# Block 0 of an adaptive-LayerNorm transformer kernel: loads, LayerNorm 1 and queue order rearranged

## The chip, the cores and the metric

One core of a Trainium2 chip runs the whole program. The metric is the device time of one execution in microseconds (us); smaller is better. Three executions of the kernel before took 597.66, 599.33 and 599.54 us, median 599.33.

Names used below: PE is TensorE (matrix products), with PEld its weight loads; DVE is VectorE; ACT is ScalarE; POOL is GpSimd; SP is SyncE, which here only issues DMA transfers. PSUM is the memory that PE writes its sums to, in banks; SBUF is the memory that all engines read.

## The reference

All tensors are float32. `x` is (2, 2048, 512), `cond_1024` is (2, 512).

```python
emb = jnp.dot(jax.nn.silu(t), ada_w) + ada_b
shift_msa, scale_msa, gate_msa, shift_mlp, scale_mlp, gate_mlp = jnp.split(emb, 6, axis=-1)
norm = _ln(x) * (1.0 + scale_msa[:, None]) + shift_msa[:, None]
h = jax.nn.gelu(jnp.dot(norm, ssm_w1) + ssm_b1, approximate=False)
ssm_out = jnp.dot(h, ssm_w2) + ssm_b2
x = x + gate_msa[:, None] * ssm_out
norm2 = _ln(x) * (1.0 + scale_mlp[:, None]) + shift_mlp[:, None]
hf = jax.nn.gelu(jnp.dot(norm2, ff_w1) + ff_b1, approximate=True)
ff_out = jnp.dot(hf, ff_w2) + ff_b2
x = x + gate_mlp[:, None] * ff_out
```

`_ln` subtracts the mean and divides by sqrt(variance + 1e-6) along the last axis.

## The kernel before

The 4096 tokens are cut into 8 blocks of 512. Each block goes through four matrix products: `hA` (w1, 512 to 512), `oA` (w2, 512 to 512, added to x), `hC` (fw1, 512 to 1024) and `oC` (fw2, 1024 to 512, added to x). `hA` and `oA` of a block are each done by a seven-product scheme: instead of eight products of half-size blocks there are seven, P1 to P7, on sums and differences of quarters. The sums of activations are `nS` (for w1's input) and `hSA` (for w2's input); the sums of weights are `w_s` and `fw_s`. Four sums belong to each operand: the first (s0), the second (s1), one written over a quarter in place, and the third (s2). P5 needs s0, P6 needs s1, P7 the quarter in place. For activations of blocks 0 and 1 DVE makes them, for weights POOL does (both L340, two SBUF operands).

PE accumulates P1, P6, P7 and P4 one upon the other in one PSUM bank ("y", tiles `py_...`), P5 and P3 in bank "v" (`pv_...`), P2 in bank "x" (`px_...`); each tag has two buffers. Between two products in the same bank, the earlier result has to be read out (`after` in `hidden` and `residual`) before PE may add the next. `hidden` reads `hA` with the bias b1 added (L594, on DVE, or on ACT when `on_act` is set, L592), adds (L600, L607, L610, on DVE) and applies GELU on ACT. `residual` adds products to x on DVE (L642).

Every engine has one queue and works it in order; the kernel is written under a manual schedule, so the order of the Python statements is the order of each queue. `hooks` (L435) put extra work behind a named product: `hook(hooks, ("P5", "P4"), ops)` runs the first op after P5 is issued and all the rest after P4.

Block 0 starts so. ACT loads four small tables of rows; SP loads x of block 0 in two halves, then `ada_0`, `ada_1` (columns of ada_w for shift and scale, 1 MB each), `w1` (1 MB), `ada_2`, `w2`, gate biases, x of block 1, `ada_3`, `ada_4`, `fw1`. DVE takes mean and variance of the four slots of x (L454, L455), POOL and DVE turn them into `rstd` and `nmr` (`scales`), ACT and DVE normalize two slots each (`normal`, L494 and L498) into `blocks`; PE transposes them (L523); ACT and DVE apply shift and scale (`modulate`, L537 and L539) into `nT`. The shift and scale come from `modulation`: 16 small products on PE (L267, tile `pada`), a transposition (L283) and an addition (L287) on DVE. `gate_rows_of(2)` does the same for the gate (pada_2, `grows`, L295), `first_ssm_gate` spreads it over partitions on PE (`pgate`, L302), `fold2` multiplies w2 by it on DVE (L388) and then makes w2's sums on POOL, and `biases` adds gate times b2 (`gb`) to the four slots of x on POOL (L654).

In the result the order on PE in block 0 is: pada_0, pada_1, 16 transposes, P1, P2, pada_2, P5, pgate, P6, P3, P7, pada_3, P4 of `hA_0`; then P1, P2, P5, P6, pada_4, P7, P3, P4 of `oA_0`, with the transposes of block 1 around P4; then `hA_1`, whose order is P1, P2, P5, P6, pada_5, P7, P3, P4.

Of the kernel before, what the change touches and what calls it, by code (L numbers as in the profile page):

```python
# [36 lines left out]
F32 = mybir.dt.float32  # L37
AF = mybir.ActivationFunctionType
ALU = mybir.AluOpType
EPS = 1e-06  # L40
# [100 lines left out]
def kernel(  # L141
# [29 lines left out]
    const = ctx.enter_context(tc.tile_pool(name="const", bufs=1))  # L171
# [14 lines left out]
    G = 32  # L186
# [3 lines left out]
    R_COND, R_ADA = 0, B * KD  # L190
# [3 lines left out]
    def big_tile(name):  # L194
        return big.tile([P, KD, D], F32, tag="big", name=name)
# [8 lines left out]

    ada = {}

    def load_ada(g):
        ada[g] = big_tile(f"ada_{g}")
        nc.sync.dma_start(
            out=ada[g], in_=ada_w[:, g * D : (g + 1) * D].rearrange("(k p) n -> p k n", p=P)  # L210
        )

    def load_w(name, w, t=None, eng=nc.sync):
        if t is None:
            t = const.tile([P, w.shape[0] // P, w.shape[1]], F32, tag=name, name=name)
        eng.dma_start(out=t, in_=w.rearrange("(k p) n -> p k n", p=P))
        return t
# [13 lines left out]
    ident = const.tile([P, P], F32, tag="ident", name="ident")  # L231
    make_identity(nc, ident)
    load_x(0, 2)
    load_ada(0)
    load_ada(1)
    w1_sb = load_w("w1", w1)
    load_ada(2)

    nc.gpsimd.memset(brows[:, :2, :P], 0.0)
# [12 lines left out]
    b2_bc = work.tile([P, D], F32, tag="gb", name="gb2_0", bufs=2)  # L252
# [3 lines left out]
    load_ada(4)  # L256
    fw1_sb = load_w("fw1", fw1)

    mods = {}

    def rows_of(g):

        pa = ps_g.tile([P, D], F32, tag="x", name=f"pada_{g}")
        w = ada[g].rearrange("p k (n m q) -> p k m n q", n=KD, q=G)
        for k in range(KD):
            for m in range(P // G):
                nc.tensor.matmul(  # L267
                    pa[m * G : (m + 1) * G, :P],
                    silu[:, k, :],
                    w[:, k, m],  # L270
                    start=(k == 0),
                    stop=(k == KD - 1),
                    tile_position=(0, m * G),
                    skip_group_check=True,
                )
        return pa

    def modulation(g0, part):

        g = g0 + part  # L280
        pa = rows_of(g)
        turned = pa[:, P : 2 * P]
        nc.vector.transpose(turned, pa[:, :P])  # L283
        turned = turned.rearrange("p (n q) -> p n q", n=KD)
        m = const.tile([P, KD, B], F32, tag=f"mod_{g0}_{part}", name=f"mod_{g0}_{part}")
        bias = colsT[:, R_ADA + g * KD : R_ADA + (g + 1) * KD]
        nc.vector.tensor_tensor(m, turned[:, :, :B], bias.unsqueeze(2).to_broadcast([P, KD, B]), ALU.add)  # L287
        mods[g0, part] = m

    gate, gate_rows = {}, {}  # L290

    def gate_rows_of(g, tag):
        pa = rows_of(g)
        r = work.tile([P, P] if g == 2 else [P, D], F32, tag=tag, name=f"grows_{g}", bufs=1)
        nc.vector.tensor_tensor(r[:, :P], pa[:, :P], gate_b[g], ALU.add)  # L295
        gate_rows[g] = r
# [138 lines left out]
    def hook(hooks, places, ops):  # L435

        for n, op in enumerate(ops):
            hooks.setdefault(places[min(n, len(places) - 1)], []).append(op)


    class Norm:
# [17 lines left out]
        def scales(self, on_dve=False):  # L459
# [20 lines left out]
            v.tensor_tensor(self.nmr, self.mv[:, :, 0], self.rstd, ALU.mult)  # L480
            v.tensor_scalar(self.nmr, self.nmr, -1.0, None, ALU.mult)  # L481

        def blocks(self):
            return work.tile([P, C, KD, C, Q], F32, tag="blocks", name=f"blocks{self.name}")

        def normal(self, c, eng=None, on_pe=False):

            if c == 0:
                self.nT = big_tile(f"nT{self.name}")
                self.xn = self.blocks().rearrange("p m k c q -> p m (k c q)") if on_pe else self.nT  # L490
            t = self.xn[:, c, :]
            x_c = xs[self.i][:, c, :]
            if eng is None:
                nc.scalar.activation(  # L494
                    t, x_c, AF.Identity, bias=self.nmr[:, c : c + 1], scale=self.rstd[:, c : c + 1]
                )
            else:
                eng.tensor_scalar(  # L498
                    t, x_c, self.rstd[:, c : c + 1], self.nmr[:, c : c + 1], ALU.mult, ALU.add
                )  # L500
# [150 lines left out]
    def biases(i, gb):  # L651

        return [
            lambda c=c: nc.gpsimd.tensor_tensor(xs[i][:, c, :], xs[i][:, c, :], gb, ALU.add)  # L654
            for c in range(C)
        ]
# [9 lines left out]

    forms = const.tile([P, 16, C, HT // C], F32, tag="forms", name="forms")

    hA_0 = forms[:, :8].rearrange("p n a r -> p (n a r)").rearrange("p (k t) -> p k t", k=KD)

    def sums_of_registers(program, reg, engs):

# [105 lines left out]
    def run(ops):  # L778
        for op in ops:
            op()  # L780
# [13 lines left out]
    colsT = const.tile([P, ROWS], F32, tag="colsT", name="colsT")  # L794
# [5 lines left out]
    for n in range(IDLE):  # L800
# [3 lines left out]
            idle, ident, ident.unsqueeze(1).to_broadcast([P, C, P]), start=True, stop=True  # L804
        )

    run(n1[0].stats())
    nc.vector.tensor_copy(colsT, pt[:, :ROWS])


    nc.scalar.activation(
# [1 line left out]
        colsT[:, R_COND:R_ADA].rearrange("p (b k) -> p b k", b=B),  # L813
        AF.Silu,
    )

    for g in (1, 4):
        rows_g = colsT[:, R_ADA + g * KD : R_ADA + (g + 1) * KD]
        nc.vector.tensor_scalar(rows_g, rows_g, 1.0, None, ALU.add)

    picks = const.tile([P, P // G, P], F32, tag="picks", name="picks")
    nc.vector.tensor_copy(
        picks, ident.rearrange("p (m q) -> p m q", q=G)[:, :, :1].to_broadcast([P, P // G, P])
    )
    n1[0].scales(on_dve=True)

    w1_ops, w1_sums, _ = weight_of_first("w1", w1_sb)
    run(w1_sums)
    modulation(0, 0)
    for c in range(C):  # L830
        n1[0].normal(c, nc.vector if c % 2 else None, on_pe=True)
    modulation(0, 1)
    pts = {}

    def transposed(k):
        pts[k] = n1[0].transpose(k, ps_g.tile([P, TB], F32, tag="yv"[k % 2], name=f"pt1_0_{k}"))

    for k in range(KD):
        transposed(k)
    for k in range(KD):  # L840
        n1[0].modulate(k, pts[k], nc.vector if k % 2 else None)
    n1_sums = n1[0].summed(nc.vector)
    run(n1_sums[:2])
    load_ada(5)
# [2 lines left out]
    gb, hA = {2: b2_bc}, {}  # L847
# [9 lines left out]
    def fold2(lo, hi):  # L857
        return [lambda k=k: found["w2"][1][k]() for k in range(lo, hi)]

    hooks = {}  # L860
    hook(hooks, ("P1",), n1_sums[2:3])
    hook(hooks, ("P2",), [lambda: gate_rows_of(2, "grows")] + n1_sums[3:])
    st = n1[1].stats()
    hook(hooks, ("P5",), [ssm_gate, gb2_0] + biases(0, b2_bc) + fold2(0, 1))
    hook(hooks, ("P6",), fold2(1, 7))
    hook(hooks, ("P3", "P7"), st[:2])
    hook(hooks, ("P7",), [lambda: modulation(3, 0)])
    hA[0] = First(0, n1[0].ops, hooks, ("P1", "P2", "P5", "P6", "P3", "P7", "P4"), hA_0)
    w2_ops = found["w2"][0]

    hA_sums = hA[0].summed(nc.vector)
    run(hA_sums[:2])
    hooks = {}
    hook(hooks, ("P1",), hA_sums[2:3] + st[2:] + [n1[1].scales] + fold2(7, 8))
    hook(hooks, ("P2",), hA_sums[3:] + [lambda c=c: n1[1].normal(c, on_pe=True) for c in range(C)])
    hook(hooks, ("P6",), [lambda: modulation(3, 1)])
    hook(hooks, ("P3", "P3", "P4"), n1[1].turned())
    n2 = {0: Norm(0, 2)}
    st = n2[0].stats()
    hook(hooks, ("P3",), st[:2])  # L880
    fw1_ops, fw1_sums, fw1_s = weight_of_first("fw1", fw1_sb)
    hook(hooks, ("P2",), fw1_sums[:1])
    hook(hooks, ("P5", "P4"), fw1_sums[1:3])
    residual("oA_0", 0, hA[0], w2_ops, KD // 2, hooks, order=FIRST)

    def ff_gate():
# [10 lines left out]
    n1_sums = n1[1].summed(nc.vector)  # L897
    run(st[2:3] + n1_sums[:2] + st[3:])
    hooks = {}
# [18 lines left out]
    st = n1[2].stats()  # L918
    hooks = {}
# [15 lines left out]
    hooks = {}  # L935
# [27 lines left out]
    hooks = {}  # L963
# [10 lines left out]
    hooks = {}  # L974
# [6 lines left out]
    hooks = {}  # L981
# [11 lines left out]
    for i in range(1, NBLK):  # L993
        nxt, nx2, last = i + 1 < NBLK, i + 2 < NBLK, i + 1 == NBLK
        hC = Second(i)
        hooks = {}
# [21 lines left out]
        hooks = {}  # L1018
# [16 lines left out]
        hooks = {}  # L1035
# [58 lines left out]
        hooks = {}  # L1094
# [52 lines left out]
```

## Time and profile before

| what | us |
|---|---|
| median of three executions | 599.33 |
| the profiled execution, whole | 597.58 |
| its span, first to last instruction | 595.8 |
| PE busy in it | 588.3 (99%) |
| POOL busy | 395.6 (66%) |
| DVE busy | 372.9 (63%) |
| ACT busy | 220.2 (37%) |

The profile is of one execution. Its times count from the first instruction. The timeline lists instructions in order of time: start, duration, engine, line of the kernel, operation, output and inputs, the count of merged instructions, and in brackets the idle time before and what ended it. An instruction of 128x512 elements works on 128 partitions with 512 numbers each. A float32 matrix product appears as two records; "x8" is one of the seven products of a block. PE's records overlap, since it is pipelined: the next product starts before the one before has left.

Times on which later sections rest, from the transfers' records: x of block 0 landed at 4.72 and 6.36, ada_0 at 9.10, ada_1 at 11.80, w1 at 14.51, ada_2 at 17.23, w2 at 20.67, x of block 1 at 23.87.

### The profile page before, as it was taken

The page shows a single profiled execution, that of the slowest core. Times are in us where ns is not written, and L with a number is a line of the kernel's source. Part 1 is how long each engine was busy: PE and PEld are TensorE (multiplying, and loading weights), DVE is VectorE, ACT ScalarE, POOL GpSimd, SP SyncE. Part 2 cuts the span into 40 slices and gives each one's busy share as a digit, 9 for nine tenths or more (in the row PEclk, how much of TensorE's full clock was granted, in tenths as well). Part 3 has the DMA queues.
Part 4 walks back from the last instruction along what each step waited for, and adds up shares of the span by engine and source line. Part 5 has one row for each costly group of instructions (what it writes and reads, how often), then busy time and mean ns, then how long its engine had stood idle before and what let it go on. Part 6 is the DMA issues. An engine that isn't in the chain of part 4 may idle for free.

```text
span 595.8 us, 8294 instructions
## 1 busy us (share of the span) xinstructions
PE 588.3 (99%) x2875; PEld 510.6 (86%) x2875; DVE 372.9 (63%) x637; ACT 220.2 (37%) x366; POOL 395.6 (66%) x465
## 2 busy tenths in 40 slices
PE   7999999999999999999999999999999999999997
PEld 4888888888888888888888888888888888888886
DVE  4978988897554475555754468643655236458642
ACT  3234437305432364234721356232543235212410
POOL 1878489999853994649967499957975696440300
PEclk9999999999999999999999999999999999999999
DMA  8990332200324105340143601331030400031001
GB/s 319 396 380 11 82 71 82 97 36 35 72 72 136 24 0 136 123 131 1 23 138 70 212 1 45 98 87 55 1 70 2 128 15 2 0 70 73 1 1 71
DMA packets 23702, 50.13 MB, mean 84 GB/s; under 512 B 4544, under 2 KB 5100, under 8 KB 22764
## 3 DMA queue, kind: packets, MB, share of 16 engines
q1 hardware_dynamic: 20624, 45.38, 24.0%
q10 hardware_dynamic: 3036, 4.22, 3.0%
q8 instruction: 23, 0.38, 0.3%
q14 instruction: 19, 0.16, 0.1%
HBM read 26.51 MB, written 8.40 MB: 59 GB/s over the span
## 4 chain that ended last, share of the span: by engine, by line
PE 97%; DMA 2%; DVE 1%; SPq 0%; issue 0%
PE py_oC L420 19%; PE px_hC L741 10%; PE py_oA L420 9%; PE pv_oC L420 9%; PE py_hA L420 9%; PE py_hC L741 8%; PE pv_hC L741 8%; PE pv_oA L420 5%; PE px_oC L420 5%; PE pv_hA L420 4%; PE py_hC L420 2%; PE px_oA L420 2%; PE px_hA L420 2%; DMA ada<-in_L_cond_ada_w_dram 2%; PE pv_hC L420 1%; PE pada L267 1%
## 5 line engine op out<-in xcount | busy, mean ns | idle before, releaser
L654 POOL TENSOR_TENSOR x<-x,gb 128x512 f32<-128x512 f32 x64 | 79.5, 1277 | 5.3 <-issue 2.1
L537 ACT ACTIVATE nT<-nT,mod,mod 128x512 f32<-128x512 f32 x54 | 39.6, 802 | 102.0 <-DMA nT<-blocks 95.9
L463 POOL TENSOR_SCALAR ve<-mv 128x4 f32<-128x4 f32 x16 | 3.7, 232 | 91.7 <-DVE mv L455 85.0
L494 ACT ACTIVATE nT<-x,nmr,rstd 128x512 f32<-128x512 f32 x56 | 42.4, 803 | 52.4 <-POOL nmr L481 36.6
L420 PE MATMUL py_oC<-fw,hClo 128*128 128x256 f32 x256 | 57.9, 379 | 0.0
L420 PEld LDWEIGHTS py_oC<-fw,hClo 128*128 128x128 f32 x256 | 48.6, 190 | 6.6
L642 DVE TENSOR_TENSOR x<-py_oC,x 128x512 f32<-128x512 f32 (+1 forms) x36 | 22.6, 629 | 42.9 <-PE py_oC L420 42.9
L454 DVE BATCH_NORM_STATS2 st<-x 128x6 f32<-128x512 f32 x64 | 43.5, 679 | 5.0 <-DMA x<-in_x_dram 4.7
L340 POOL TENSOR_TENSOR hSC<-hClo,hChi 128x512 f32<-128x512 f32 (+1 forms) x17 | 20.1, 1188 | 39.7 <-ACT hChi L736 29.2
L741 PE MATMUL py_hC<-forms,fw 128*128 128x256 f32 x168 | 40.8, 379 | 0.0
L758 DVE TENSOR_TENSOR hClo<-hClo,py_hC 128x512 f32<-128x512 f32 x42 | 28.5, 681 | 16.9 <-ACT hClo L755 10.4
L505 DVE STREAM_TRANSPOSE blocks<-nT 128x512 f32<-128x512 f32 x56 | 37.8, 694 | 1.3 <-ACT nT L494 0.9
L679 POOL TENSOR_TENSOR forms<-forms 128x256 f32<-128x256 f32 x48 | 35.7, 743 | 2.8
L741 PEld LDWEIGHTS py_hC<-forms,fw 128*128 128x128 f32 x168 | 31.8, 190 | 4.4
L758 DVE TENSOR_TENSOR hChi<-hChi,pv_hC 128x512 f32<-128x512 f32 x35 | 23.3, 683 | 17.1 <-PE pv_hC L741 14.2
L642 DVE TENSOR_TENSOR x<-py_oA,x 128x512 f32<-128x512 f32 x32 | 22.0, 688 | 18.9 <-PE py_oA L420 18.3
L420 PE MATMUL py_hA<-nT,w 128*128 128x256 f32 x128 | 30.4, 380 | 0.0
L736 ACT ACTIVATE hClo<-hClo,colsT 128x256 f32<-128x256 f32 x56 | 25.4, 500 | 10.8 <-DVE hClo L758 10.7
L420 PE MATMUL px_oC<-fw,hChi 128*128 128x256 f32 x128 | 28.9, 379 | 0.0
L420 PE MATMUL py_oC<-fw_s,hSC 128*128 128x256 f32 x128 | 28.9, 379 | 0.0
L420 PE MATMUL pv_oC<-fw,hSC 128*128 128x256 f32 x128 | 28.9, 379 | 0.0
L420 PE MATMUL pv_oC<-fw_s,hSC 128*128 128x256 f32 x128 | 28.9, 379 | 0.0
(213 smaller groups left out, 1424.8 us busy)
## 6 DMA issues: line engine op xcount, KB each, us to landing
nT<-blocks SPq DMA_DIRECT2D x168, 64.0 KB
out_dram<-x SPq DMA_DIRECT2D x15, 512.0 KB
x<-in_x_dram SPq DMA_DIRECT2D x7, 1024.0 KB
ada<-in_L_cond_ada_w_dram SPq DMA_DIRECT2D x6, 1024.0 KB
fw<-in_L_cond_ff_w_dram SPq DMA_DIRECT2D x3, 2048.0 KB
nT<-blocks ACTq DMA_DIRECT2D x56, 64.0 KB
w<-in_L_cond_ssm_w_dram SPq DMA_DIRECT2D x3, 1024.0 KB
x<-in_x_dram SPq DMA_DIRECT2D x2, 512.0 KB
```

Source lines behind the costliest of these rows:

```text
L340: eng.tensor_tensor(out[:, r], a[:, r], b[:, r], f)
L420: nc.tensor.matmul(ps[b][j * apart][:, j, :], lhs(p, j, k), rhs(p, j, k), start=(fresh and j * (not apart) == 0 and k == 0), stop=(p in (" ...
L454: nc.vector.bn_stats(st, xs[self.i][:, c, :])
L494: nc.scalar.activation(t, x_c, AF.Identity, bias=self.nmr[:, c : c + 1], scale=self.rstd[:, c : c + 1])
L505: nc.vector.transpose(self.bl[:, :, :, c, :].rearrange("p m k q -> p k m q"), self.nT[:, c, :].rearrange("p (k m q) -> p k m q", k=KD, m=C),)
L537: nc.scalar.activation(dst, src, AF.Identity, bias=shift, scale=scale)
L642: nc.vector.tensor_tensor(d, ps[BANK[p]][:, js], d, ALU.add)
L654: lambda c=c: nc.gpsimd.tensor_tensor(xs[i][:, c, :], xs[i][:, c, :], gb, ALU.add)
L679: eng.tensor_tensor(reg[d], reg[a], reg[b], ALU.add if f == "+" else ALU.subtract)
L736: nc.scalar.activation(h, h, AF.Gelu_apprx_tanh, bias=fb1T[:, m : m + 1])
L741: nc.tensor.matmul(ps[b][:, j, :], fa[ra][:, j * P : (j + 1) * P], fb[rb].rearrange("p a (c q) -> p c a q", q=Q), start=(fresh and j == 0) ...
L758: nc.vector.tensor_tensor(dest(d), dest(d), ps[b], op)
```

## The change

Loads: `ada_0` and `ada_1` come in column halves, in the order ada_0 first half, ada_1 first half, ada_0 second half, ada_1 second half; w1 in two column halves. Modulation of LayerNorm 1 is done in halves of its four column groups: half 0 gives shift and scale for k = 0, 1, half 1 for k = 2, 3. The scales of block 0 are made for two slots at a time (`scales_of`). ACT normalizes slots 0 and 1, DVE slots 2 and 3. `nT` of block 0 lies in the upper half of `forms` instead of a buffer of its own.

Queues: `hA_0` now runs in the order P1, P2, P5, pada_2, P6, pgate, P7, P3, P4, with `on_act=True`; `pada_3` moves from `hA_0` to `oA_0` behind P6, `pada_4` from there to behind P4 and the last transposes. The products of gate and b2 and the four `biases` of block 0 move from P5 of `hA_0` to P5, P6 and P7 of `oA_0`, so on POOL they stand behind w2's sums and LayerNorm 1's scales of block 1. fw1's first three sums move from P2, P5 and P4 of `oA_0` to P7, P3 and P4: on POOL they still stand directly before LayerNorm 2's scales of block 0, now behind the biases.

```diff
-    def load_ada(g):
-        ada[g] = big_tile(f"ada_{g}")
+    def load_ada(g, half=None):
+        if not half:
+            ada[g] = big_tile(f"ada_{g}")
+        c = slice(0, D) if half is None else slice(half * D // 2, (half + 1) * D // 2)
         nc.sync.dma_start(
-            out=ada[g], in_=ada_w[:, g * D : (g + 1) * D].rearrange("(k p) n -> p k n", p=P)
+            out=ada[g][:, :, c], in_=ada_w[:, g * D : (g + 1) * D][:, c].rearrange("(k p) n -> p k n", p=P)
         )
...
-    load_ada(0)
-    load_ada(1)
-    w1_sb = load_w("w1", w1)
+    for half in range(2):
+        load_ada(0, half)
+        load_ada(1, half)
+    w1_sb = const.tile([P, KD, D], F32, tag="w1", name="w1")
+    for c in (slice(0, D // 2), slice(D // 2, D)):
+        nc.sync.dma_start(out=w1_sb[:, :, c], in_=w1[:, c].rearrange("(k p) n -> p k n", p=P))
     load_ada(2)
...
+    def modulation(g0, part, half=None):
...
+        n = slice(0, KD) if half is None else slice(half * KD // 2, (half + 1) * KD // 2)
+        pa = pada[g][:, n.start * G : n.stop * G]
...
+        for k in range(KD):
+            for m in range(P // G):
+                nc.tensor.matmul(
+                    pa[m * G : (m + 1) * G, :],
+                    silu[:, k, :],
+                    w[:, k, m, n],
...
+        def finish():
+            nc.vector.transpose(turned, pa)
+            to = mods[g0, part][:, n]
...
+        if half is not None:
+            return finish
+        finish()
...
+        def scales_of(self, s):
...
+            nc.gpsimd.tensor_scalar(ve, self.mv[:, s, 1], EPS, None, ALU.add)
+            nc.gpsimd.tensor_tensor(r, ve, minus_half[:, s], ALU.pow)
+
+            def rest():
+                v.tensor_tensor(e, r, ve, ALU.mult)
+                v.scalar_tensor_tensor(e, e, -0.5, r, ALU.mult, ALU.mult)
+                v.scalar_tensor_tensor(self.rstd[:, s], e, 1.5, r, ALU.add, ALU.mult)
...
-    run(n1[0].stats())
+    st = n1[0].stats()
+    run(st[:2])
+    scales_lo = n1[0].scales_of(halves[0])
+    run(st[2:])
     nc.vector.tensor_copy(colsT, pt[:, :ROWS])
+    scales_hi = n1[0].scales_of(halves[1])
+    scales_lo()
...
+    for c in (0, 1):
+        n1[0].normal(c, on_pe=True)
...
+    scales_hi()
+    for c in (2, 3):
+        n1[0].normal(c, nc.vector, on_pe=True)
+    w1_ops, w1_sums, _ = weight_of_first("w1", w1_sb)
+    run(w1_sums)
...
+    for finish in [modulation(0, part, 0) for part in range(2)]:
+        finish()
+    for k in range(KD):
+        transposed(k, (0, 1))
+    for k in range(KD):
+        transposed(k, (2, 3))
+    n1[0].modulate(0, pts[0])
+    n1[0].modulate(1, pts[1], nc.vector)
...
+    for finish in [modulation(0, part, 1) for part in range(2)]:
+        finish()
+    n1[0].modulate(2, pts[2])
+    n1[0].modulate(3, pts[3], nc.vector)
...
-    hook(hooks, ("P2",), [lambda: gate_rows_of(2, "grows")] + n1_sums[3:])
+    hook(hooks, ("P2",), n1_sums[3:])
     st = n1[1].stats()
-    hook(hooks, ("P5",), [ssm_gate, gb2_0] + biases(0, b2_bc) + fold2(0, 1))
-    hook(hooks, ("P6",), fold2(1, 7))
-    hook(hooks, ("P3", "P7"), st[:2])
-    hook(hooks, ("P7",), [lambda: modulation(3, 0)])
-    hA[0] = First(0, n1[0].ops, hooks, ("P1", "P2", "P5", "P6", "P3", "P7", "P4"), hA_0)
+    hook(hooks, ("P5",), [lambda: gate_rows_of(2, "grows")])
+    gb2 = biases(0, b2_bc)
+    hook(hooks, ("P6",), [ssm_gate] + fold2(0, 2))
+    hook(hooks, ("P7",), fold2(2, 7))
+    hook(hooks, ("P3", "P4"), st[:2])
+    hA[0] = First(0, n1[0].ops, hooks, FIRST, hA_0, on_act=True)
...
+    hook(hooks, ("P5",), [gb2_0])
+    hook(hooks, ("P6",), gb2[:2])
+    hook(hooks, ("P7",), gb2[2:])
     hook(hooks, ("P2",), hA_sums[3:] + [lambda c=c: n1[1].normal(c, on_pe=True) for c in range(C)])
-    hook(hooks, ("P6",), [lambda: modulation(3, 1)])
+    hook(hooks, ("P6",), [lambda: modulation(3, 0)])
     hook(hooks, ("P3", "P3", "P4"), n1[1].turned())
+    hook(hooks, ("P4",), [lambda: modulation(3, 1)])
...
-    hook(hooks, ("P2",), fw1_sums[:1])
-    hook(hooks, ("P5", "P4"), fw1_sums[1:3])
+    hook(hooks, ("P7", "P3", "P4"), fw1_sums[:3])
```

The order of instructions that the changed program has on DVE at the turn from block 0 to block 1 is: the addition of `oA_0`'s P4 to x, pada_4's transposition and addition, statistics of x slot 2, nS s0, nS s1, statistics of x slot 3, the reading of `hA_1`'s P1, nS's quarter in place. In the kernel before, pada_4's two instructions stand earlier and the rest is the same.

More of the change, by code (lines that the diff above doesn't have):

```diff
@@ L257 @@
     fw1_sb = load_w("fw1", fw1)
-    mods = {}
+    mods, pada = {}, {}
+    def modulation(g0, part, half=None):
+        g = g0 + part
+        if not half:
+            pada[g] = ps_g.tile([P, D], F32, tag="x", name=f"pada_{g}")
+            mods[g0, part] = const.tile([P, KD, B], F32, tag=f"mod_{g0}_{part}", name=f"mod_{g0}_{part}")
+        n = slice(0, KD) if half is None else slice(half * KD // 2, (half + 1) * KD // 2)
+        pa = pada[g][:, n.start * G : n.stop * G]
+        w = ada[g].rearrange("p k (n m q) -> p k m n q", n=KD, q=G)
+        for k in range(KD):
[4 more added lines that the diff above has]
+                    w[:, k, m, n],
+                    start=(k == 0),
+                    stop=(k == KD - 1),
+                    tile_position=(0, m * G),
+                    skip_group_check=True,
+                )
+        turned = pada[g][:, P + n.start * G : P + n.stop * G]
+        bias = colsT[:, R_ADA + g * KD : R_ADA + (g + 1) * KD][:, n]
+        def finish():
+            nc.vector.transpose(turned, pa)
+            to = mods[g0, part][:, n]
+            by_n = turned.rearrange("p (n q) -> p n q", q=G)
+            nc.vector.tensor_tensor(
+                to, by_n[:, :, :B], bias.unsqueeze(2).to_broadcast([P, n.stop - n.start, B]), ALU.add
+            )
+        if half is not None:
+            return finish
+        finish()
+    gate, gate_rows = {}, {}
     def rows_of(g):
@@ L276, in rows_of @@
         return pa
[L278 to L290, printed above, removed]
     def gate_rows_of(g, tag):
@@ L481, in scales @@
             v.tensor_scalar(self.nmr, self.nmr, -1.0, None, ALU.mult)
+        def scales_of(self, s):
+            n, v = f"{self.name}_{s.start}", nc.vector
+            if s.start == 0:
+                self.rstd = small.tile([P, C], F32, tag="rstd", name=f"rstd{self.name}")
+                self.nmr = small.tile([P, C], F32, tag="nmr", name=f"nmr{self.name}")
+            ve, r, e = [small.tile([P, C], F32, tag=k, name=f"{k}{n}")[:, s] for k in ("ve", "r", "e")]
+            nc.gpsimd.tensor_scalar(ve, self.mv[:, s, 1], EPS, None, ALU.add)
[4 more added lines that the diff above has]
+                v.scalar_tensor_tensor(self.rstd[:, s], e, 1.5, r, ALU.add, ALU.mult)
+                v.scalar_tensor_tensor(
+                    self.nmr[:, s], self.mv[:, s, 0], -1.0, self.rstd[:, s], ALU.mult, ALU.mult
+                )
+            return rest
         def blocks(self):
@@ L488, in normal @@
             if c == 0:
-                self.nT = big_tile(f"nT{self.name}")
+                self.nT = nT_0 if self.name == "1_0" else big_tile(f"nT{self.name}")
                 self.xn = self.blocks().rearrange("p m k c q -> p m (k c q)") if on_pe else self.nT
@@ L667 @@
     forms = const.tile([P, 16, C, HT // C], F32, tag="forms", name="forms")
-    hA_0 = forms[:, :8].rearrange("p n a r -> p (n a r)").rearrange("p (k t) -> p k t", k=KD)
+    hA_0, nT_0 = [
+        forms[:, n : n + 8].rearrange("p n a r -> p (n a r)").rearrange("p (k t) -> p k t", k=KD)
+        for n in (0, 8)
+    ]
     def sums_of_registers(program, reg, engs):
@@ L805 @@
         )
-    run(n1[0].stats())
+    halves = slice(0, C // 2), slice(C // 2, C)
+    st = n1[0].stats()
+    run(st[:2])
+    scales_lo = n1[0].scales_of(halves[0])
+    run(st[2:])
     nc.vector.tensor_copy(colsT, pt[:, :ROWS])
+    scales_hi = n1[0].scales_of(halves[1])
+    scales_lo()
     nc.scalar.activation(
@@ L819, with transposed @@
         nc.vector.tensor_scalar(rows_g, rows_g, 1.0, None, ALU.add)
+    scales_hi()
[3 more added lines that the diff above has]
+    run(w1_sums)
+    pts = {k: ps_g.tile([P, TB], F32, tag="yv"[k % 2], name=f"pt1_0_{k}") for k in range(KD)}
+    def transposed(k, slots):
+        for c in slots:
+            nc.tensor.transpose(pts[k][:, c * P : (c + 1) * P], n1[0].xn[:, c, k * P : (k + 1) * P], ident)
+    for finish in [modulation(0, part, 0) for part in range(2)]:
[6 more added lines that the diff above has]
+    n1[0].modulate(1, pts[1], nc.vector)
     picks = const.tile([P, P // G, P], F32, tag="picks", name="picks")
@@ L824 @@
     )
[L825 to L841, printed above, removed]
+    for finish in [modulation(0, part, 1) for part in range(2)]:
+        finish()
+    n1[0].modulate(2, pts[2])
+    n1[0].modulate(3, pts[3], nc.vector)
     n1_sums = n1[0].summed(nc.vector)
```

## The prediction

> **What bounds the kernel now.** First the busy slices and the chain that ended last, on the page.
>
> ```profile
> PE   7999999999999999999999999999999999999997
> ...
> PE 97%; DMA 2%; DVE 1%; SPq 0%; issue 0%
> ```
>
> PE is the bound and idles at the start alone; so next its timeline there.
>
> ```profile
> 9.23 1.08 PE L267 MATMUL pada<-ada,silu 128*32 128x128 f32 x32 [0.48 <-DMA ada<-in_L_cond_ada_w_dram]
> 11.84 1.08 PE L267 MATMUL pada<-ada,silu 128*32 128x128 f32 x32 [1.53 <-DMA ada<-in_L_cond_ada_w_dram]
> 12.85 1.96 PE L523 MATMUL pt<-ident,blocks 128*128 128x128 f32 x16
> 14.65 1.95 PE L420 MATMUL py_hA<-nT,w 128*128 128x256 f32 x8
> ```
>
> P1 starts at 14.65, 0.14 after w1 landed (14.51). Behind it I looked for products that start late against the one before: the worst is 0.25 us late, all together 2.1 us. So the whole gain to be had is an earlier P1, and every new wait of PE costs its full length.
>
> Then the places where POOL and DVE both work on two SBUF operands (L340), at the turn to block 1; first DVE, then POOL, then PE.
>
> ```profile
> 29.55 1.59 DVE L340 TENSOR_TENSOR hSA<-forms 128x512 f32<-128x512 f32 x1
> ...
> 46.21 1.48 DVE L340 TENSOR_TENSOR nS<-nT 128x512 f32<-128x512 f32 x1
> 47.79 0.69 DVE L340 TENSOR_TENSOR nS<-nT,nS 128x512 f32<-128x512 f32 x1
> 48.40 0.69 DVE L454 BATCH_NORM_STATS2 st<-x 128x6 f32<-128x512 f32 x1
> ...
> 49.22 0.67 DVE L594 TENSOR_TENSOR hA<-py_hA,colsT 128x512 f32<-128x512 f32 x1
> ```
> ```profile
> 29.33 1.27 POOL L340 TENSOR_TENSOR w_s<-w,w_s 128x512 f32<-128x512 f32 x1
> ...
> 44.78 2.36 POOL L340 TENSOR_TENSOR fw<-fw 128x1024 f32<-128x1024 f32 x1
> 49.39 0.23 POOL L463 TENSOR_SCALAR ve<-mv 128x4 f32<-128x4 f32 x1 [2.25 <-DVE mv L455]
> ```
> ```profile
> 50.51 1.89 PE L420 MATMUL py_hA<-nS,w_s 128*128 128x256 f32 x8
> ```
>
> A DVE sum beside no POOL sum takes 0.69. The one at 46.21 began while POOL's fw1 sum ran (to 47.14) and ended at 47.69, 0.55 behind it; the one at 29.55 ended at 31.14, 0.55 behind POOL's (30.59). All eight such pairs before 61 us ended 0.55 apart: DVE waits until POOL's instruction is over. POOL's next one then takes 0.45 longer (1.72 for 1.27). Statistics, additions from PSUM and the folds of w2 keep their 0.68 beside POOL. PE at 50.51 is `hA_1`'s P6, which needs P1 read out of its bank (L594, ended 49.89): 0.6 of slack.
>
> **The change, part by part.**
>
> *Start.* The packets of the 2 KB loads filled the queues at 1 MB per 2.70 us. Now 3 MB go in 1 KB pieces. The nearest 1 KB packets are the last stores to out: 48 ns each, against 84 to 89 ns for 2 KB loads; at worst then 32 packets per queue and half, 1.54 us a half; at best half of 2.70, 1.35. From 6.36 (x landed), the second halves of ada_0 and ada_1 land at 10.98 and 12.52 (10.4, 11.8), the first half of w1 at 14.06 (13.1), the second at 15.6 (14.5). I take the store row.
> The Trainium skill, "DMA: Bandwidth & Descriptors", Specifications, puts line rate at 512 B and more, which makes 1 KB pieces free: an estimate of 13.1 for w1's half instead of 14.06. No load of 1 KB is in this trace.
>
> PE's side: normals end about 11.4 (DVE's scales still wait for POOL's power at 9.7, as before, then 0.75, then two normals 0.99), transposes end 12.35 (half of them, 0.9, behind that), then two half sets of pada. A set of 16 takes 1.01 from start to start; half the columns but all its 32 weight loads: 0.50 to 1.01 each, and I take 0.88 (32 loads of 110 ns in four column groups). End 14.1. Modulation of k = 0, 1 is done by 13.15 (two DVE pairs of 0.44, then 0.85). So P1 starts at 14.2, both paths agreeing; bounds 13.4 and 14.5. Gain 0.45 (0.15 to 1.25). P2, at 15.9, needs k = 2 and 3: 14.1 + 0.1 + 0.44 + 0.85 = 15.5.
> Then DVE's and POOL's sums for block 0 take turns as shown above: POOL begins at 15.65 and ends its four at 17.45, 19.2, 20.9 and 22.6, DVE's s1, quarter and s2 end 0.55 behind the first three, `grows` at 21.75. P5 (17.7), P6 (20.4), pgate (22.2), P7 and P3 find them done; the nearest is `grows`, 0.45 ahead.
>
> *Block 0 on PE.* P1 to `oA_0`'s P1 was 15.64 (14.65 to 30.29). pada_3 leaves (1.0), and so does P4's wait for DVE behind it (0.17). P7 now comes right behind pgate, and needs P6 read by ACT: two readings 0.84 begin 0.2 after pgate starts, pgate covers 0.89, so P7 waits about 0.25 (0 to 0.4). 14.72: `oA_0` at 28.9. The next 15.04 (30.29 to 45.33) grow by one pada, 1.1, since pada_3 takes pada_4's place and pada_4 follows P4. `hA_1`'s P1: 45.05, 0.28 ahead of before.
> DVE loses three readings of 0.68 to ACT, whose 0.84 each fit idle time (3.9 and 6.0 us before its GELUs). The table load of 1.28 goes behind P1's reading, at 16.9; GELU waits for DVE until 20. Without that cover it costs P7 nothing, its operand is another.
> Halved scales, three more small DVE sets and nT's new place lie in time before P1 that is counted above; three more SP issues (0.4 to 0.8 each) stand behind transfers queued for over 5 us.
> ada_2 lands at 18.3, wanted at 19.4; w2 at 21.8, wanted at 23.2: covered, 1 us each.
>
> *Block 1's transposes.* They follow P3 of `oA_0`, and before they had no slack at all: the chain from POOL's scales over ACT's normals ended at 41.78, PE came at 41.85.
>
> ```profile
> 35.72 0.23 POOL L463 TENSOR_SCALAR ve<-mv 128x4 f32<-128x4 f32 x1 [3.45 <-DVE mv L455]
> ...
> 38.57 0.25 POOL L481 TENSOR_SCALAR nmr<-nmr 128x4 f32<-128x4 f32 x1
> ```
> ```profile
> 38.85 2.93 ACT L494 ACTIVATE blocks<-x,nmr,rstd 128x512 f32<-128x512 f32 x4 [7.52 <-POOL nmr L481]
> ```
> ```profile
> 41.85 1.04 PE L523 MATMUL pt<-ident,blocks 128*128 128x128 f32 x8
> ```
>
> Now PE is there at 40.5 (28.9 and the 11.56 from 30.29 to 41.85). DVE: pgate ends 23.2, four folds and two readings to 27.75, statistics to 29.3, hSA s0 (POOL's w2 sum ends 29.7) 30.25, s1 30.9, then as before 2.85 to the last mean, 33.75. POOL's scales and ACT's normals take 6.15: 39.9. No wait; 0.5 of slack (0.6 late at the far bound, if s1 also meets a POOL sum).
>
> *Biases behind w2's sums.* Before, the biases ran ahead of w2's sums, at a time when DVE had PSUM work only:
>
> ```profile
> 23.03 4.98 POOL L654 TENSOR_TENSOR x<-x,gb 128x512 f32<-128x512 f32 x4 [2.13 <-issue]
> ...
> 40.01 2.37 POOL L340 TENSOR_TENSOR fw_s<-fw 128x1024 f32<-128x1024 f32 x1
> 42.46 2.37 POOL L340 TENSOR_TENSOR fw_s<-fw_s,fw 128x1024 f32<-128x1024 f32 x1
> ```
>
> Now POOL has scales to 36.95, w2's s2 (1.27) to 38.2, four biases (4.98) to 43.2, then fw1's sums, 2.36 each: 43.2 to 45.55, to 47.9, to 50.3. In the kernel before these ended at 47.14. x's additions of P3 and P4 wait for the biases to 40.7 and 43.2, and PE gives them at 40.6 and 43.25: nothing.
> DVE behind `oA_0`: pada_4 is turned at 45.15 (P1 plus 0.1), addition, statistics (0.81), nS s0 asked for at 46.5, inside POOL's second sum: ends 48.45. POOL's third has begun at 47.9 and lasts to 50.7 (0.45 longer). nS s1 waits for it: 51.25. Statistics 52.05, then P1's reading ends 52.7. Queued behind it on DVE are the quarter in place, P2's addition and the scales of LayerNorm 2; waiting for it is P6: 52.75 instead of 50.51. P5 (48.5) just gets its s0.
>
> Sum: +2.24 us. That is -0.45 +0.25 -0.17 +0.1 (one pada costs 1.1 for 1.0) and 2.5 of waiting at P6.
>
> *Later.* LayerNorm 2's scales of block 0 begin at 52.1 (49.39): 0.5 later than PE is; hSA s1 had 0.65 of slack before `oA_1`'s P6 (61.45, 62.10), nS2 1.45 before `hC`'s (73.06, 74.51). Hidden; gone, at most 0.3.
> The skill, "SBUF — State Buffer", in the section on two separate sides, lets any POOL instruction that reads SBUF lock the pair. The row says less: hSA took 0.68 at 36.12 beside POOL's power on 128x4 (36.03 to 37.07). By the page the quarter in place would end near 54.1, not 53.3, behind P6 all the same: the sum stays.
>
> **The rivals.**
> *The sums meet otherwise.* The step rests on nS s0 falling into the second sum, with 1 us to both sides. If POOL is over 1 us later, or over 1.4 earlier, only one sum of 2.36 or less has to be waited for: P6 waits 1.1 to 1.3, total +0.9. For it: two chains of twenty steps each; against: both start from the same pgate.
> *The head start stands* (not slower). Needs nS s1 done by 49.1, so that P6 is not later than 0.28 behind its own time. Then -0.28, at best -1.1 (P1 at 13.4). For it: DVE met one fw1 sum before and had 0.6 to spare. Against: POOL gets 4.98 more work ahead of them. 599.0, at best 598.2.
> *Slower still.* 1 KB loads above 48 ns, or the transposes 0.6 late and P1 at 14.5: +3.2, 602.5. Against: the store row and ACT's slack.
>
> **How the numbers follow.** The sum is made on the span of 595.8: 598.0, and 597.58 becomes 599.8. This execution lies with the lowest of the three (597.66); the two others and the median lie 1.75 above. Results are medians: 599.33 + 2.24 = 601.5. Range 598.4 (the +0.9 case on the lower level) to 602.8. A measurement here can tell 0.3%, 1.8 us, from no change.
> Chances: forecast 0.53, met otherwise 0.19, head start stands 0.18, slower still 0.08, nothing at all 0.02. Slower by over 0.3%: 0.47 + 0.03 + 0.08 = 0.58. Faster: only the head start, with the level's luck, 0.08. Within: 0.34.
>
> **What would show it.** PE's P1 at 14.2, w1's halves landing near 14.1 and 15.6; P7 of `hA_0` 0.25 behind pgate; fw1's sums on POOL from 43.2 on; at the turn two nS sums on DVE that take near 2 and 2.8 us; P6 of `hA_1` at 52.75, its gap ended by DVE. Wrong if nS s1 takes 0.7, or if P6 comes before 50.6.

## The result, and the profile after

| | before | after |
|---|---|---|
| median of six executions each, us | 598.08 | 601.38 |
| ratio, 95% interval | | 1.0051, 1.0038 to 1.0063 |
| profiled execution, span | 595.8 | 598.4 |
| last matrix product ends | 591.84 | 595.07 |

The change makes the kernel slower, by more than the 0.3% that can be told from nothing. Most executions of both kernels lie on one of two levels some 1.7 us apart (before 597.7 and 599.4, after 600.6 and 602.3), the upper one at a granted clock of 0.996 to 0.997, so the spans of two executions of the lower level are compared: by them the change costs 2.6 us.

The page of the kernel after: PE's busy slices, and the chain that ended last.

```profile
PE   8998999999999999999999999999999999999997
...
PE 92%; DVE 4%; DMA 2%; issue 1%; POOL 1%; ACT 0%; ACTq 0%; DVEq 0%; POOLq 0%
```

PE is still the bound, but of the chain 92% is PE's where it was 97%: DVE and POOL now stand in it. Where, PE's timeline after says (L278 is pada, L449 the products; lines moved from L267 and L420).

```profile
9.19 1.10 PE L278 MATMUL pada<-ada,silu 128*32 128x64 f32 x64
...
12.50 1.10 PE L278 MATMUL pada<-ada,silu 128*32 128x64 f32 x64
14.09 1.97 PE L449 MATMUL py_hA<-forms,w 128*128 128x256 f32 x8 [0.49 <-DMA w<-in_L_cond_ssm_w_dram]
...
37.23 1.96 PE L449 MATMUL py_oA<-w,forms 128*128 128x256 f32 x8 [0.47 <-DVE x L691]
...
52.96 1.99 PE L449 MATMUL py_hA<-nS,w_s 128*128 128x256 f32 x8 [2.18 <-DVE hA L643]
```

P1 of `hA_0` starts 0.56 earlier than before. Then waits appear that the kernel before didn't have; the two longest are 0.47 at P7 of `oA_0` and 2.18 at P6 of `hA_1`. (A number in brackets is the time in which PE stands idle. Counted from start to start against the usual distance, a product is late by some 0.07 to 0.17 more, since it usually starts before the one before has left; where a product is called late, this is meant.) Behind the second wait, DVE and POOL of the kernel after (L643 reads `hA`'s product, formerly L594):

```profile
46.74 1.99 DVE L369 TENSOR_TENSOR nS<-nT 128x512 f32<-128x512 f32 x1
48.84 2.66 DVE L369 TENSOR_TENSOR nS<-nT,nS 128x512 f32<-128x512 f32 x1
...
52.23 0.67 DVE L643 TENSOR_TENSOR hA<-py_hA,colsT 128x512 f32<-128x512 f32 x1
```
```profile
43.39 2.37 POOL L369 TENSOR_TENSOR fw_s<-fw 128x1024 f32<-128x1024 f32 x1
45.84 2.34 POOL L369 TENSOR_TENSOR fw_s<-fw_s,fw 128x1024 f32<-128x1024 f32 x1
48.15 2.80 POOL L369 TENSOR_TENSOR fw<-fw 128x1024 f32<-128x1024 f32 x1
```

nS s0 is asked for inside POOL's second fw1 sum (45.84 to 48.18) and ends at 48.73, 0.55 behind it; nS s1 is asked for inside the third (to 50.95) and ends at 51.50, again 0.55 behind. In the kernel before these two took 1.48 and 0.69. Below, this is called the lock: a DVE sum of two SBUF operands that meets a running POOL sum is over 0.55 after that sum.

How PE stands against the kernel before, by the starts of its products: -0.56 at P1 of `hA_0`, +0.01 at P1 of `hA_1`, +2.45 at its P6, +3.01 at P6 of `oA_1`, +3.23 at the last product's end. The span grows by only 2.6: from the last product to the end there are 3.96 us before and 3.3 after, a stretch that holds the last addition and the last store and that is between 3.3 and 4.0 in all the profiles of this case.

### The profile page after: what moved, and what is told of

Same layout as the page of the kernel before. It is cut to its first block, busy times and chain, and to the rows that moved or that the text cites. A ratio compares the mean times of both kernels' runs of the same rounds, so it can differ in the third digit from the quotient of the medians.

```text
span 598.4 us, 8442 instructions
## 1 busy us (share of the span) xinstructions
PE 590.0 (99%) x2939; PEld 510.9 (85%) x2939; DVE 373.9 (62%) x642; ACT 222.6 (37%) x372; POOL 395.5 (66%) x467
## 4 chain that ended last, share of the span: by engine, by line
PE 92%; DVE 4%; DMA 2%; issue 1%; POOL 1%; ACT 0%; ACTq 0%; DVEq 0%; POOLq 0%
PE py_oC L449 18%; PE px_hC L793 10%; PE pv_oC L449 9%; PE py_oA L449 8%; PE py_hC L793 8%; PE pv_hC L793 8%; PE py_hA L449 8%; PE px_oC L449 5%; PE pv_oA L449 4%; PE pv_hA L449 4%; PE py_hC L449 2%; PE px_hA L449 2%; PE px_oA L449 2%; DMA w<-in_L_cond_ssm_w_dram 1%; PE pv_hC L449 1%; DVE hSA L369 1%
## 5 line engine op out<-in xcount | busy, mean ns | idle before, releaser
L449 PE MATMUL py_oC<-fw,hClo 128*128 128x256 f32 x256 | 57.9, 379 | 0.0
L449 PEld LDWEIGHTS py_oC<-fw,hClo 128*128 128x128 f32 x256 | 48.6, 190 | 6.6
L449 PE MATMUL pv_oC<-fw_s,hSC 128*128 128x256 f32 x128 | 28.9, 379 | 0.0
L449 PE MATMUL py_oC<-fw_s,hChi 128*128 128x256 f32 x128 | 28.9, 379 | 0.0
L449 PE MATMUL py_oC<-fw_s,hSC 128*128 128x256 f32 x128 | 28.9, 379 | 0.0
L449 PE MATMUL pv_oC<-fw,hSC 128*128 128x256 f32 x128 | 28.9, 379 | 0.0
L449 PE MATMUL px_oC<-fw,hChi 128*128 128x256 f32 x128 | 28.9, 379 | 0.0
```

Of the source, the lines that this page charges most:

```text
L449: nc.tensor.matmul(ps[b][j * apart][:, j, :], lhs(p, j, k), rhs(p, j, k), start=(fresh and j * (not apart) == 0 and k == 0), stop=(p in (" ...
```

## The experiments

Theory: POOL's biases stand behind w2's sums, so fw1's sums come 3.4 us later, and nS s0 and s1 each wait until a whole one is over. Rival: the lateness at P6 comes from DVE's own order (pada_4's two instructions now stand directly before the statistics and nS). A second rival was the start itself, with its 1 KB loads. Each kernel below is an edit of the kernel after unless another is named, each was timed beside the kernel before, and a ratio is to that one.

**The third sum of fw1 later.** It goes from in front of LayerNorm 2's scales to the fourth, behind the biases of block 1; DVE's order stays.

```diff
-    hook(hooks, ("P7", "P3", "P4"), fw1_sums[:3])
+    hook(hooks, ("P7", "P3"), fw1_sums[:2])
...
-    hook(hooks, ("P1",), hA_sums[2:3] + fw1_sums[3:])
+    hook(hooks, ("P1",), hA_sums[2:3] + fw1_sums[2:])
```

> fw1's third sum goes on POOL from directly behind the second to directly before the fourth (behind LayerNorm 2's scales and the biases of block 1); DVE's and PE's orders stay those of the changed kernel. Theory (DVE's two-SBUF sums wait for POOL's running instruction): nS s0 still takes 2.0, nS s1 takes 0.7, P6 of hA_1 waits about 0.4 instead of 2.18; but the third and fourth sums now run back to back from 58.9 and meet both hSA sums of block 1, so oA_1's P6 waits about 2.1 where it waited 0.42. Span near 598.3: the wait moves. Rival (DVE is late because pada_4's turning now stands in front of the statistics and nS): P6 of hA_1 still waits 2.2, nothing new at oA_1, span 598.4.

Measured: 600.29 us, ratio 1.0032 (1.0019 to 1.0045). DVE's timeline, then POOL's and PE's:

```profile
46.89 2.00 DVE L369 TENSOR_TENSOR nS<-nT 128x512 f32<-128x512 f32 x1
48.99 0.69 DVE L369 TENSOR_TENSOR nS<-nT,nS 128x512 f32<-128x512 f32 x1
...
61.95 2.72 DVE L369 TENSOR_TENSOR hSA<-hSA,hA 128x512 f32<-128x512 f32 x1
```
```profile
59.00 2.36 POOL L369 TENSOR_TENSOR fw<-fw 128x1024 f32<-128x1024 f32 x1
61.31 2.80 POOL L369 TENSOR_TENSOR fw_s<-fw,fw_s 128x1024 f32<-128x1024 f32 x1
```
```profile
51.15 1.99 PE L449 MATMUL py_hA<-nS,w_s 128*128 128x256 f32 x8 [0.21 <-DVE hA L643]
...
65.32 1.99 PE L449 MATMUL py_oA<-w_s,hSA 128*128 128x256 f32 x8 [2.27 <-DVE x L691]
```

nS s1 is back at 0.69 and P6 of `hA_1` waits 0.21, with pada_4 still where the change put it: the rival about DVE's order falls. The wait has followed POOL's sum to `hSA`, where two sums in a row (59.00 to 64.11) hold s0 and s1, and P6 of `oA_1` waits 2.27. So the sums are the cause, and they need another place or another size.

**The sums of fw1 in pieces.** Each of the four is issued as four instructions of 128x256 numbers.

```diff
+            for r in [slice(c * n, (c + 1) * n) for c in range(4)]:
+                eng.tensor_tensor(out[:, :, r], a[:, :, r], b[:, :, r], f)
```

> fw1's four sums are each cut into four pieces of 128x256, same places and order. Theory: a DVE sum waits for a piece of about 0.7 at most, so nS s0 and s1 take 0.7 to 1.3 each and P6 of hA_1 waits under 0.3; POOL's own end of the three sums stays near 52, so LayerNorm 2's chain is as late as in the changed kernel while PE comes 2 us earlier, and hC's first or third product waits 1 to 2. Span 597 to 598. Rival (DVE's order): P6 of hA_1 waits 2.2 as before, span 598.4 or more.

Measured: 601.20 us, ratio 1.0044 (1.0030 to 1.0058). DVE, then PE:

```profile
46.77 0.69 DVE L369 TENSOR_TENSOR nS<-nT 128x512 f32<-128x512 f32 x1
47.56 1.03 DVE L369 TENSOR_TENSOR nS<-nT,nS 128x512 f32<-128x512 f32 x1
```
```profile
59.66 1.99 PE L464 MATMUL py_hA<-nS,w 128*128 128x256 f32 x8 [2.39 <-DVE hA L671]
```

nS's sums now take 0.69 and 1.03 and P6 doesn't wait, though POOL works at the same sums the whole time: DVE gets in between two pieces. But the time is not won. POOL pays instead, 2.81, 3.70 and 3.75 for the three sums where whole ones took 2.37, 2.34 and 2.80, and begins LayerNorm 2's scales at 53.66. ACT's normals start at 56.76, DVE's turns of them wait for that, and the reading of P7 behind them comes so late that P4 of `hA_1` waits 2.39. That miss was mine: I had looked for the wait at `hC` alone, where P6 waits 0.94 besides. POOL's lateness before the scales is a second limit; the pieces let its sums end 2.6 us later, on top of the 3.4 by which the biases had moved fw1's sums.

**The biases in front of w2's sums**, where they stood before; all else of the change stays.

```diff
-    hook(hooks, ("P6",), [ssm_gate] + fold2(0, 2))
+    hook(hooks, ("P6",), [ssm_gate, gb2_0] + gb2 + fold2(0, 2))
```

> Undoes one part: gate times b2 and the four biases of block 0 stand again in front of w2's sums; all else as in the changed kernel. Theory: fw1's sums end on POOL before nS is asked for, both nS sums take 0.7, P6 of hA_1 has no wait; but w2's sums run 4 to 5 us later and meet hSA s0, s1 and the quarter, the last mean of block 1 comes at about 36.0 for 33.93, and the transposes wait 1.4 to 1.8 for ACT's normals. Span near 597.2. Rival (DVE's order): P6 of hA_1 waits 2.2 as before, span 598.4 or more.

Measured: 599.34 us, ratio 1.0019 (1.0006 to 1.0031). DVE, then PE:

```profile
31.12 1.64 DVE L369 TENSOR_TENSOR hSA<-hSA,forms 128x512 f32<-128x512 f32 x1
...
48.08 0.66 DVE L369 TENSOR_TENSOR nS<-nT 128x512 f32<-128x512 f32 x1
```
```profile
38.57 1.97 PE L449 MATMUL py_oA<-w,forms 128*128 128x256 f32 x8 [1.67 <-DVE x L691]
```

Undoing this one part takes the wait at P6 away. The price is the same lock at another place: w2's sums (29.27 to 33.89) now meet `hSA`'s sums, the last mean of block 1 comes at 36.05 instead of 34.1, and P7 of `oA_0` waits 1.67 for DVE's reading. I had expected that wait at the transposes, which start behind it without one. (P6 of `hC` waits 0.69 besides; that wait is taken up in the next experiment.) So moving the biases does remove a wait; it carries 5 us of POOL from one crossing of DVE and POOL to the next.

**The second and third sums of fw1 left out.**

```diff
-    hook(hooks, ("P7", "P3", "P4"), fw1_sums[:3])
+    nc.gpsimd.memset(fw1_s[:, 1], 0.0)
...
+    hook(hooks, ("P7",), fw1_sums[:1])
```

> Leaves out the second and third sums of fw1 (part of the fw1 product is computed from zeros and unsummed weights); orders on DVE and PE are those of the changed kernel. Theory: both nS sums take 0.7, P6 of hA_1 has no wait, and oA_1's P6 waits at most 0.1; span near 595.8, time 2.6 under the changed kernel and level with before. Rival (DVE's order): P6 still waits 2.2, span 598.4. If waits of about 1 us stay, both take part.

Measured: 598.10 us, ratio 0.9998 (0.9987 to 1.0008), span 596.2. DVE:

```profile
46.93 0.66 DVE L369 TENSOR_TENSOR nS<-nT 128x512 f32<-128x512 f32 x1
47.69 0.69 DVE L369 TENSOR_TENSOR nS<-nT,nS 128x512 f32<-128x512 f32 x1
```

nS's sums take 0.66 and 0.69, P6 of `hA_1` has no wait, and with the ratio down from 1.0051 some 3.2 us are back. The wait of 0.47 at P7 of `oA_0` is still there, and there is one that I hadn't expected, at P6 of `hC`, which is 0.86 late:

```profile
75.39 1.97 PE L449 MATMUL py_hC<-nS,fw_s 128*128 128x256 f32 x8 [0.69 <-DVE hClo L643]
```

DVE's reading in front of it stands behind the folds of fw2, which wait for gate 5: SP issues its load at 67.29 (before 66.16), though the first of the four gate stores in front of it is issued at nearly the same time (62.70 and 62.42). The load waits for these stores to complete.

**The start alone**, with everything behind it in the order of before: biases in front of w2's sums, pada_2 behind P2, no readings on ACT.

```diff
-    hook(hooks, ("P5",), [lambda: gate_rows_of(2, "grows")])
+    hook(hooks, ("P2",), [lambda: gate_rows_of(2, "grows")] + n1_sums[3:])
...
-    hook(hooks, ("P6",), [ssm_gate] + fold2(0, 2))
+    hook(hooks, ("P5",), [ssm_gate, gb2_0] + biases(0, b2_bc) + fold2(0, 1))
```

> The changed start (ada_0, ada_1 and w1 loaded in halves, LayerNorm 1 of block 0 in halves, its normalized block in the forms) with everything behind it in the order of before: POOL's biases in front of w2's sums, pada_2 behind P2, ScalarE reads nothing for hA_0. Theory (POOL's biases behind w2's sums hold VectorE's sums of nS, the start itself gives half a microsecond): P1 of hA_0 starts at 14.1 as in the changed kernel, P6 of hA_1 has no wait of 2 us, the two sums of nS take no more than 1.5 and 0.7. But pada_2 now follows P2 at 17.6 and its load lands at 18.3 to 19.2, so P5 is up to 1 us late and most of the head start is lost there: span 595.6 to 596.9, ratio 0.999 to 1.002. Rival (the start or its 1 KB loads cost the time): 598 or more, whatever the order behind.

Measured: 598.57 us, ratio 1.0007 (0.9998 to 1.0016), span 596.6. PE:

```profile
14.69 1.97 PE L449 MATMUL py_hA<-forms,w 128*128 128x256 f32 x8 [0.84 <-DMA w<-in_L_cond_ssm_w_dram]
...
19.51 1.08 PE L310 MATMUL pada<-ada,silu 128*32 128x128 f32 x32 [1.13 <-DMA ada<-in_L_cond_ada_w_dram]
```

The rival about the start (598 or more in the span) falls. P1 is no earlier in this one profile, because x's second half landed at 6.88 and not at 6.4 to 6.5 as in the nine other profiles of the changed start, where P1 starts at 14.09 to 14.28. It would have mattered little: pada_2, at its old place, waits for ada_2 to 19.4, and even in the kernel after, with x on time, ada_2 lands at 19.13, where pada_2 started at 18.27 before. So with these loads an earlier start is worth nothing without a later pada_2.

**The gate's stores earlier**, in the kernel that leaves the sums out: they are issued right behind the rows of the gate, not behind the moves of LayerNorm 2.

```diff
-    hook(hooks, ("P6",), [lambda: gate_rows_of(5, "g5")])
+    hook(hooks, ("P6",), [lambda: gate_rows_of(5, "g5"), lambda: store_gates(5)])
```

> The kernel that leaves out fw1's second and third sums, with the gate's four stores issued right behind the rows of the gate (at about 56) and not behind the moves of LayerNorm 2. Theory (in it the last 0.86 is the gate's load, which the store's completion holds until 67.3): the load is issued at about 62.5 to 63, the copy of the gate on ScalarE at 69.0, hC's P6 no wait: span 595.2 to 595.5, ratio 0.998 to 0.9995. Rival (the wait at hC's P6 comes from VectorE's own work or ScalarE's): copy earlier, wait stays near 0.8, span 596.0 to 596.4.

Measured: 597.79 us, ratio 0.9992 (0.9983 to 1.0001), span 596.0. The load is issued at 62.63 as expected, but P6 of `hC` is still 0.67 late where it was 0.86. ACT's timeline says why:

```profile
67.20 2.93 ACT L586 ACTIVATE nT<-nT,mod,mod 128x512 f32<-128x512 f32 x4 [7.37 <-DMA nT<-blocks]
```

These are the shifts of `nT`, in front of the gate's copy on ACT. They wait for the moves until 67.20, and with the stores in their old place until 65.93. The load's 256 KB now lie between the moves (the copies out of `blocks` into `nT`, 16 transfers of 64 KB). Half right: the load was late because of the stores, but once it is early it seems to stand in the way; the last experiment below tests that.

**All waits mended, in three steps.** The first step: the product of gate and b2 behind w2's first two folds; one bias in POOL's gap between w2's first two sums, one in front of block 1's scales, two behind w2's last sum; fw1's third and fourth sum in four pieces; P6 of `hA_0` read on DVE; the gate's stores early.

```diff
+    hook(hooks, ("P6",), [ssm_gate] + fold2(0, 2) + [gb2_0])
+    hook(hooks, ("P7",), fold2(2, 5) + gb2[:1] + fold2(5, 7))
...
+    hook(hooks, ("P6",), gb2[2:])
```

> The changed kernel with each wait that the experiments showed taken away: gate times bias right behind w2's first two folds on VectorE, one of block 0's bias turns in POOL's gap between w2's first two sums and one in front of block 1's scales, the other two behind w2's last sum; the third and fourth sums of fw1 in four pieces each; P6 of hA_0 read on VectorE; the gate's stores issued before the moves of block 0's LayerNorm 2. Theory: fw1's first two sums stand at 41.0 to 45.8, the third in pieces beside nS, so nS's sums take under 1.1 each, P6 of hA_1 no wait, oA_0's P7 no wait, hA_0's P7 under 0.1, hC's P6 no wait; the head start of 0.5 at P1 stands to the end: span 594.9 to 595.4, ratio 0.9985 to 0.9995. Rival (POOL's early bias turns delay block 1's last mean by more than the 0.5 of slack in front of its transposes, or the sums in pieces make POOL late at hC): a new wait of 0.5 to 1.5, span 595.7 to 596.7, ratio 1.000 to 1.0015.

Measured: 598.18 us, ratio 0.9997 (0.9988 to 1.0006). The waits at P6 of `hA_1`, P7 of `oA_0` and P6 of `oA_1` are gone, that at P7 of `hA_0` fell from 0.25 to 0.1. Two are there: P4 of `oA_0` is 0.64 late, since DVE's reading of P7 stands behind both late biases of the same rows of x; and P6 of `hC` is 0.86 late, by the moves as in the last experiment. The second step, an edit of the first, orders the biases by the rows that each reading needs and puts the gate's copy in front of the shifts:

```diff
-    hook(hooks, ("P6",), gb2[2:])
+    hook(hooks, ("P6",), gb2[:1])
+    hook(hooks, ("P7",), gb2[2:3])
...
-    hook(hooks, ("P6",), n2[0].moved() + [ff_gate])
+    hook(hooks, ("P6",), [ff_gate] + n2[0].moved())
```

> e6_all_mended with its two new waits taken away: the bias turns in another order (the fourth tile in POOL's gap, the second in front of block 1's scales, the first behind w2's last sum, the third behind VectorE's reading of P7 of oA_0), and ScalarE's copy of the gate in front of its four shifts of nT. Theory: the last product of oA_0 (P4, at 41.7 in e6) has no wait, since no reading of VectorE stands behind two bias turns any more (0.64 back); the gate's copy comes at 65 to 66.5 where it came at 70.4, VectorE's folds follow it, and hC's P6 has no wait (0.86 back): last matmul at 591.3 to 591.8, span 594.9 to 595.5, ratio 0.9975 to 0.9995. Rival (block 2's normals, which start at 73.6 where they started at 71.9 before, or fw1's first sum at 41.2, are late for something else): one of the waits stays or a new one of 0.3 to 1 appears, span 595.6 to 596.4, ratio 0.999 to 1.001.

Measured: 597.06 us, ratio 0.9987 (0.9978 to 0.9996). P4 of `oA_0` has no wait. P6 of `hC` is 0.55 late, no longer by DVE but by POOL's nS sum, which the late shifts (67.00) hold up. So the third step, an edit of the second, issues the gate's load on ACT's queue behind its moves, with the copy again behind the shifts:

```diff
+    nc.scalar.dma_start(out=t, in_=gates_dram[5][0].unsqueeze(0).to_broadcast([P, D]))
```

> e8_mended_again with the load of gate 5 issued on ScalarE's queue behind its eight moves of LayerNorm 2 (not on SP's, between them), and the copy of the gate again behind the four shifts of nT. Theory (in e8 the load's 256 KB land between the moves and make them 1.2 us late, so POOL's sums of nS start late and hC's P6 waits 0.55): the shifts of nT start at 65.2 to 66.0 where they started at 67.0, the copy at 68.2 to 69.2, POOL's nS s1 starts at 71.2 to 71.9, hC's P6 waits under 0.2: last matmul at 591.2 to 591.5, span 594.5 to 594.9, ratio 0.997 to 0.9995. Rival (VectorE's readings behind the later copy, or the moves late for another reason): hC's P6 waits 0.4 to 0.9, span 595.0 to 595.6.

Measured: 596.16 us, ratio 0.9970 (0.9960 to 0.9981), span 594.4: faster than both kernels, though by only as much as can be told (the slowest of its eight executions took 596.41, the fastest of the kernel before beside it 597.65). PE's timeline, then ACT's:

```profile
14.14 1.97 PE L466 MATMUL py_hA<-forms,w 128*128 128x256 f32 x8 [0.73 <-DMA w<-in_L_cond_ssm_w_dram]
...
36.59 1.99 PE L466 MATMUL py_oA<-w,forms 128*128 128x256 f32 x8
...
50.02 1.89 PE L466 MATMUL py_hA<-nS,w_s 128*128 128x256 f32 x8
```
```profile
65.28 2.93 ACT L603 ACTIVATE nT<-nT,mod,mod 128x512 f32<-128x512 f32 x4 [6.11 <-DMA nT<-blocks]
```

The three places of this study: P1 starts 0.51 earlier than before, P7 of `oA_0` and P6 of `hA_1` show no bracket, and no product behind P1 is late by more than 0.17. The shifts of `nT` start 1.7 earlier than in the step before, with the load behind the moves: it did stand in their way. The last product ends at 590.69, 1.16 earlier than before: the head start of 0.51, a delay of 0.3 in `hC` (at 81.87 before) that is gone, and small rests.

## Why the prediction was right, and where it wasn't

*The turn to block 1*, the step that decides, held nearly line by line: fw1's sums from 43.39 (43.2 predicted), nS s0 over at 48.73 (48.45), s1 at 51.50 (51.25), the reading at 52.90 (52.7), P6 at 52.96 (52.75). P6 itself stands still for 2.34 there; 2.5 was predicted. The experiments show the cause from three sides: moving a sum, cutting it, leaving it out each takes the wait away (moving leaves 0.21 of it) while DVE's order is kept.

*P1* came at 14.09 (14.2 predicted), by one of the two paths alone. The loads were right: w1's first half at 13.96 (14.06), its second at 15.45 (15.6), 1 KB packets 48 ns. The page "DMA: Bandwidth & Descriptors" (Specifications) of the Trainium skill puts line rate at 512 B and more; the estimate from it had w1's half there at 13.1, and the trace is against it. PE's path was mis-sized: a half set of pada takes 0.55 and not 0.88. With half the columns and the same number of weight loads it costs half, so PE was there at 13.6.

*Block 0 on PE.* P7 of `hA_0` came 0.25 late, as predicted, and the transposes had no wait (ACT's normals over at 40.25, PE there at 40.76). ada_2 landed at 19.13, not 18.3, 3.7 us behind w1 where it had been 2.7. A transfer's landing is recorded in sixteen parts: fifteen of ada_2's were there by 18.16, close to the forecast, and the last came 0.97 later. From 15.26 to 16.31 the instruction queue of the trace had moved a packet of 16 KB beside them. In the kernel before such a packet (18.41 to 19.47) lay beside w2, whose last part came 0.75 behind the others. That the packet is the cause wasn't tested. pada_2's move behind P5 covered the lateness with 0.3 us to spare, not 1.

*What failed*: "P1 45.05, 0.28 ahead of before". P1 of `hA_1` came at 45.34. The step had counted gate times b2 as moved to `oA_0` on DVE without asking who waits there: at 35.81 its 0.6 lies in front of the reading of P6, and P7 of `oA_0` waits 0.47 (0.54 late). In the mended kernel, with that product elsewhere, P7 doesn't wait.

*Later*: "at most 0.3". P6 of `oA_1` came 0.42 late. The 0.65 of slack was read at the wrong instruction: it was counted to the end of `hSA` s1 (61.45), but P6 goes into the bank of P1, whose reading is queued behind s1. In the kernel before:

```profile
61.37 0.68 DVE L642 TENSOR_TENSOR x<-py_oA,x 128x512 f32<-128x512 f32 x1
```

That reading ended at 62.05, 0.05 in front of P6 (62.10). So there was no slack, and what DVE lost reached PE: `hSA` s0 meets POOL's fourth fw1 sum in both kernels and took 2.46 where it had taken 2.17, since it was asked for earlier within that sum.

*The sum* was +2.24; the span gave +2.6, and PE's last product +3.23, of which 0.54 and 0.42 are the two delays just named. That the span hides most of this, by an end that was 0.6 shorter, is luck. So is, in part, that the median of 601.38 lies so near 601.5: the forecast stood on the first three executions of the kernel before, whose median is 1.25 above that of all six, and between the medians of six the change is 3.3, not 2.2.

*The rivals.* The sums did not meet otherwise: nS s0 fell into the second sum, 0.9 us behind its start, as said. The head start didn't stand: P6 of `hA_1` gave back four times as much.

## What to carry to other kernels

Where a sum on one engine has to wait for a running sum on another, the place in a queue of a long instruction is a cost that no busy time shows: before moving 5 us of POOL's work, list which of POOL's long sums will then lie beside which of DVE's sums, and who waits for DVE. A sum that has to lie there can be cut into pieces, as long as the engine that pays for the cut has time in front of its next deadline. And a head start of half a microsecond is worth what the tightest of the later waits leaves of it, so each of these has to be found and loosened as well.

## What the runs showed of the hardware

- DVE's sum gets in between two POOL instructions but not within one: beside POOL sums of 128x1024 DVE's sum of 128x512 takes up to 2.72, beside pieces of 128x256 it takes 0.69 to 1.20. POOL's side of it: four pieces take 2.81 where DVE makes no sum, 3.7 to 4.2 where it makes two or three, against 2.37 for the whole one.
- The gate's four stores: from their first issue to the issue of the load behind them there are 3.74 us in the kernel before and in the one with the start alone, and 4.2 to 4.6 in the kernel after and in the first four experiments. The stores' bytes are the same. What makes the difference wasn't found.
- A load of 256 KB that falls between the 16 moves of 64 KB holds these up: from the first move's issue to the shifts that wait for the moves there are 9.7 to 9.9 us in the three kernels that have it there, and 8.2 to 8.5 in the eight that don't. Issued behind the moves, it delays nothing that PE waits for.
